# A new order of the steps between graph attention and flow attention, and other engines for two units' subtracts

## The chip, the cores and the metric

The kernel runs on one core of one Trainium2 chip. The metric is the device time of one execution in microseconds (us), as the median of several runs. The engines are TensorE (PE, with its weight load PEld), VectorE (DVE), ScalarE (ACT), GpSimd (POOL) and SyncE (SP), which issues DMAs.

## The reference, cut to what matters

Four graph layers follow each other on `x` (32 batches, 512 nodes, 64 features), each as `x = x + layer(relu(layernorm(x)))`. Layers 0 and 1 multiply with the adjacency matrix and small weights. The change concerns the end of layer 2 and the begin of layer 3:

```python
# layer 2: graph attention
Wh = einsum('bnf,of->bno', h, W)
e = leaky_relu((Wh @ a1)[:, :, None] + (Wh @ a2)[:, None, :], 0.2)
att = softmax(where(adj > 0, e, -9e15), axis=-1)
x = x + elu(einsum('bij,bjo->bio', att, Wh))
# layer 3: flow attention, 8 heads of 128, then one output attention of the same form
h = relu(layernorm(x)) @ W[head]
s = einsum('bnd,bmd->bnm', h, h) * adj
s = where(s == 0, -1e16, s)
out = einsum('bnm,bmd->bnd', softmax(s, axis=2), h) + b
```

## The kernel before

Tensors lie with 128 nodes on the partitions; 512 nodes are C = 4 blocks of 128. Layers 0 to 2 work on pairs of batches, M = 16 pairs. `slot(k)` (line 1207) is one step of a software pipeline over pairs: pair k in layer 0, k-2 in layer 1, k-4 and k-5 in layer 2. When the slots are done, pairs 10 to 15 are still on their way. What is left is issued by `drain()` (line 1315), which follows a list written out by hand, `LAST` (line 1297): each word `name_i` is a step of pair i (or of unit i of layer 3), and the words' order is the order in which PE, DVE and ACT get their instructions (`manual_schedule`, line 1439). POOL and SP are not under it in the drain.

The steps that matter, for pair i of layer 2: `flip`/`ht` transpose and copy; `e1`, `c`, `wh`, `vq` the terms of the scores; `weigh` (L1057); `sc0`, `sc1` the masked scores, four instructions of 128x512 each (L1069: `c`, `mask_t` and the result in SBUF); `acc`, `den` the weighted sums on TensorE (L1082, L1093), `kacc`, `kden` their copies to SBUF, `op`, `dps` the transposes back (L1123, L1118); `read` the quotient (L1136, L1137, L1144); `exp` and `rest` the elu and the addition to x (L1157, L1158, then L905 and two L907 that centre it for the next norm); `osq`, `ovar` square and sum. Layer 1 has `nt1`, `nt1c`, `po1a`, `z`, `nt1b`, `nt1bc`, `po1b`, `x`; norms have `n1`, `n2` (centre), `sq`, `var`, `root` (square root on ACT), `turn` (reciprocal), `relu`.

Layer 3 is a row of units, `flow`: `Heads(b, i)` treats heads 2i and 2i+1 of batch b; the first units are flow[0] = (0,0), flow[1] = (1,0), flow[2] = (0,1), flow[3] = (1,1), and so on. A unit's path: `make_g` (a product on TensorE and a copy on ACT, for two units at once), `scores(r)` for r = 0..3 (L425, two matmuls into PSUM), `maxima(r)` (L440: two VectorE instructions that negate, mask and copy the scores to SBUF and keep the row minimum `top`), `spread_out` and `spread_in` (SP: `top` to DRAM and back, broadcast to all partitions, L447 and L458), `shift(r, engine)` (the subtract of the broadcast: two of 128x512 for r = 0, L468, one of 128x1024 else, L464), `exps(r)` (ACT, L477), `join(1)` and `join(3)` (VectorE, L480: rows 1 and 0, rows 3 and 2 added), `totals` (L498), `values` (L486, into `av`), `recips` and their DMAs, `normalize` (L535). `exps(r)` of an odd r writes into a PSUM tile `e_ps` for units from EARLY = 2 on, and in place for units 0 and 1. `e_ps` and the scores share `ps_s`, a ring of two tiles.

`planned()` (line 777) makes `flow_period(t)`: one period issues steps of some ten units, each at its lag: scores of unit t and t+1, shift and exps of unit t-1, totals and values of t-2, `make_g` of t+2, `features` of later batches. Units 0 and 1 are exempt from the first of these (`t - i >= EARLY`): the list `LAST` issues them, with `topb` in `adj_t`, which layer 2 needs no more. In the kernel before the list holds all of unit 0 and unit 1 up to `j1`, both with GpSimd subtracts, and all pairs to `osq_15`. Behind the list come unit 0's totals, period 1, unit 0's values, period 2, `end_of_gat` (variance and root of pair 15, line 1428) and periods 3 and on. Batch 15's result `o_end` lies in a buffer of the tag `hs3`, its exponential in `pairs_a`.

Of the kernel before, what the change touches and what calls it, by code (L numbers as in the profile page):

```python
# [14 lines left out]
P = 128  # L15
# [7 lines left out]
def fast_form(  # L23
# [340 lines left out]
    class Pair:  # L364
# [17 lines left out]

        def make_gs(self):
            pass
# [88 lines left out]
        def exps(self, r):  # L473
            to = self.joined[r] = self.p[r]
            if r % 2 and self.at >= EARLY:
                to = self.joined[r] = ps_s.tile([P, 2, N], F32, name="e_ps", tag="s")
            nc.scalar.activation(to, self.p[r], AF.Exp, scale=-1.0)  # L477
# [59 lines left out]
    class Heads(Pair):  # L537
# [51 lines left out]
        def make_g(self):  # L589
            if self.b % 2:  # L590
                return
            pss = [acc("g_ps", [P, N]) for k in range(2)]
            for k in range(2):
# [12 lines left out]
                )  # L606
            for k in range(2):
# [169 lines left out]
    def planned(units, products):  # L777
# [7 lines left out]
        def period(t):  # L785
# [4 lines left out]
            now, ahead, last = (unit(i) if t - i >= EARLY else nothing for i in (0, -1, 1))  # L790
            summed = unit(2) if t > 2 else nothing
# [6 lines left out]
            last.exps(0)  # L798
# [6 lines left out]
            last.exps(2)  # L805
# [3 lines left out]
            odd = nc.vector if t == EARLY + 1 else nc.gpsimd  # L809
# [12 lines left out]
            last.shift(1, odd)  # L822
            last.exps(1)
# [7 lines left out]
            last.join(1)  # L831
            last.shift(3, odd)
            last.exps(3)
            unit(5).back_pool()
            unit(-2).make_gs()
            last.join(3)
# [4 lines left out]
            unit(-2).make_g()  # L841
            for step in range(3):
# [43 lines left out]
    with (  # L886
# [110 lines left out]
        class Gat:  # L997
# [134 lines left out]
            def read(self):  # L1132
# [6 lines left out]
                if self.i == LATEST:  # L1139
                    self.sq = early.tile([P, 2, C, F], F32, name="o_end", tag="hs3", bufs=2)  # L1140
# [8 lines left out]
            def exp(self):  # L1149
                self.e = pairs_a.tile([P, 2, C, F], F32, name="e", bufs=1)  # L1150
                nc.scalar.activation(self.e, self.sq, AF.Exp)
# [146 lines left out]
        grow_15 nt1bc_13 flip_12 nt1_14 ht_12 read_10 sc0_11 exp_10 po1b_13 nt1c_14 rest_10  # L1298
        e1_12 wh_12 c_12 po1a_14 vq_12 n1_15 s0_0 z_14 osq_10 sc1_11 sq1_15 x_13 acc_11
        n2_13 var1_15 sq2_13 weigh_12 var2_13 den_11 kacc_11 ovar_10 m0_0 root_0 op_11  # L1300
        nt1b_14 sc0_12 kden_11 turn_0 dps_11 relu1_15 nt1bc_14 s1_0 relu2_13 nt1_15 m1_0
        read_11 sc1_12 exp_11 flip_13 nt1c_15 po1b_14 ht_13 e1_13 rest_11 wh_13 c_13 acc_12
        vq_13 x_14 osq_11 n2_14 den_12 ovar_11 sq2_14 weigh_13 kacc_12 var2_14 s2_0 kden_12
        sc0_13 root_1 dps_12 s3_0 po1a_15 m2_0 op_12 z_15 m3_0 nt1b_15 turn_1 relu2_14
        read_12 sc1_13 flip_14 nt1bc_15 spread_0 s0_1 ht_14 exp_12 po1b_15 e1_14 x_15 acc_13
        rest_12 c_14 n2_15 osq_12 den_13 sh0_0 kacc_13 ovar_12 sq2_15 m0_1 op_13 kden_13
        sh1_0 ex0_0 dps_13 var2_15 s1_1 read_13 root_2 s2_1 m1_1 sh2_0 m2_1 s3_1 period_0
        exp_13 sh3_0 turn_2 ex2_0 wh_14 m3_1 vq_14 relu2_15 spread_1 ex1_0 sc0_14 flip_15
        ht_15 ex3_0 weigh_14 sc1_14 e1_15 wh_15 c_15 vq_15 sh0_1 rest_13 acc_14 sh1_1 ex0_1
        weigh_15 osq_13 j3_0 den_14 kacc_14 sh2_1 ovar_13 ex1_1 op_14 sc0_15 kden_14 dps_14  # L1310
        sh3_1 ex2_1 sc1_15 ex3_1 read_14 j3_1 exp_14 acc_15 rest_14 den_15 kacc_15 j1_0
        osq_14 ovar_14 op_15 kden_15 j1_1 dps_15 read_15 exp_15 rest_15 osq_15
        """

        def drain():
# [84 lines left out]
            for r in range(C):  # L1400
                do[f"s{r}"] = lambda i, r=r: flow[i].scores(r)
                do[f"m{r}"] = lambda i, r=r: flow[i].maxima(r)
                do[f"sh{r}"] = lambda i, r=r: flow[i].shift(r, nc.gpsimd)
# [3 lines left out]
            def spread(i):  # L1407
                flow[i].spread_out()
                flow[i].spread_in()

            do["spread"] = spread
            do["period"] = flow_period
# [15 lines left out]
        def end_of_gat(sp):  # L1428
            sp.add(gat[LATEST])
# [52 lines left out]
    with tc.manual_schedule(  # L1482
# [15 lines left out]
        end_of_gat(unfinished)  # L1498
        for k in range(3, len(flow) + ROOM):
# [563 lines left out]
```

## Time and profile before

| | |
|---|---|
| Median of 3 runs | 2022.88 us (2019.3, 2022.88, 2022.89) |
| The profiled execution, its own time | 2021.3 us |
| Its span, first to last instruction | 2019.4 us |
| Granted TensorE clock, mean | 0.988 |
| PE busy | 1946.5 us (96%) |
| DVE busy | 1747.8 us (87%) |
| POOL busy | 1452.9 us (72%) |
| ACT busy | 1320.8 us (65%) |
| Chain that ended last | PE 79%, POOL 7%, DVE 6%, DMA 4%, ACT 2%, issue 1% |

A line such as `L464` names a line of the kernel before. "Busy" counts an engine's instructions; a matmul that is pipelined counts as busy while it is under way. A timeline row tells start, length, engine, line, operation and tiles, and in brackets how long the engine was idle before and what ended that. The profiler's span is a little shorter than the time of the execution, which also holds what lies ahead of the first and behind the last instruction.

### The profile page before, as it was taken

Reading aid. Unit: us, or ns where it says so; the run is one execution under the profiler, and the core shown is the slowest. Engines: PE = TensorE matmul, PEld = TensorE weight load, DVE = VectorE, ACT = ScalarE, POOL = GpSimd, SP = SyncE. Lnnn points to the kernel's source line nnn. Section 1 sums busy time; section 2 is a strip of 40 time slices with the busy share of each in tenths; the row PEclk is TensorE's granted clock in tenths of the full one; section 3 lists DMA queues with packets and bytes.
Section 4 is the critical chain, followed back from the end, with each engine's and each line's share of the span. In section 5 each row is a group of like instructions: output and inputs, shape, how many; then the busy total and the mean of one; then the engine's idle time right before and its main releaser. Section 6 shows DMA issues by size and latency. Waiting matters only on the chain.

```text
span 2019.4 us, 29031 instructions
## 1 busy us (share of the span) xinstructions
PE 1946.5 (96%) x9338; PEld 729.7 (36%) x9338; DVE 1747.8 (87%) x4104; ACT 1320.8 (65%) x2008; POOL 1452.9 (72%) x837
## 2 busy tenths in 40 slices
PE   7999999868999999999999999999999999999995
PEld 4655554322333333333333333333333333333232
DVE  6799987987889898988988898888888888888994
ACT  3545655446777677777776767777776776766674
POOL 2000000226989999989898989898898888889996
PEclk9999999888999999999999999999999999999998
DMA  4000000002232232323223323332222223222223
GB/s 124 1 1 1 1 1 1 11 12 68 77 79 77 75 85 76 84 71 86 74 77 80 80 70 86 75 75 80 75 70 75 75 76 76 73 77 78 77 75 82
DMA packets 185874, 128.03 MB, mean 63 GB/s; under 512 B 124985, under 2 KB 130273, under 8 KB 185585
## 3 DMA queue, kind: packets, MB, share of 16 engines
q1 hardware_dynamic: 166480, 125.30, 23.2%
q10 hardware_dynamic: 18720, 0.59, 0.5%
q8 instruction: 75, 1.23, 0.3%
q14 instruction: 87, 0.70, 0.1%
q0 software_dynamic: 512, 0.20, 0.1%
HBM read 119.48 MB, written 5.37 MB: 62 GB/s over the span
## 4 chain that ended last, share of the span: by engine, by line
PE 79%; POOL 7%; DVE 6%; DMA 4%; ACT 2%; issue 1%; SPq 0%; ACTq 0%; POOLq 0%; DVEq 0%
PE s_ps L425 22%; PE av L486 20%; PE nt_ps L966 8%; PE tot_ps L498 6%; PE y_ps L616 5%; PE gT_ps L661 5%; PE g_ps L598 3%; POOL p_att L464 3%; PE acc L1082 2%; DMA topb<-top_row 2%; POOL row L464 2%; PE po L988 1%; DVE s L1069 1%; PE den L1093 1%; DVE p_att L440 1%
## 5 line engine op out<-in xcount | busy, mean ns | idle before, releaser
L425 PE MATMUL s_ps<-g,hx 64*128 64x512 f32 x2048 | 519.5, 618 | 12.4 <-DVE p_att L480 5.8
L464 POOL TENSOR_TENSOR row<-row,topb 128x1024 f32<-128x1024 f32 x182 | 430.5, 2388 | 0.0
L464 POOL TENSOR_TENSOR p_att<-p_att,topb 128x1024 f32<-128x1024 f32 x182 | 429.6, 2383 | 0.0
L440 DVE CUSTOM_DVE_ANT_0 p_att<-s_ps,flow_neg 128x512 f32<-128x512 f32 x492 | 310.0, 686 | 43.7 <-PE s_ps L425 42.8
L440 DVE CUSTOM_DVE_ANT_0 row<-s_ps,flow_neg 128x512 f32<-128x512 f32 x496 | 312.5, 685 | 39.1 <-PE s_ps L425 38.9
L425 PEld LDWEIGHTS s_ps<-g,hx 64*128 64x128 f32 x2048 | 176.3, 187 | 323.4 <-DVE top L440 175.9
L468 POOL TENSOR_TENSOR p_att<-p_att,topb 128x512 f32<-128x512 f32 x124 | 155.6, 1277 | 94.4 <-DMA topb<-top_row 80.5
L1211 POOL TENSOR_TENSOR x<-x,bias_b 128x512 f32<-128x512 f32 x16 | 20.3, 1274 | 255.1 <-DVE hn L907 255.1
L468 POOL TENSOR_TENSOR row<-row,topb 128x512 f32<-128x512 f32 x120 | 150.9, 1279 | 63.8 <-DMA topb<-top_row 49.3
L610 ACT COPY g<-g_ps 128x512 f32<-128x512 f32 x128 | 132.1, 1140 | 94.4 <-PE g_ps L598 94.3
L634 DVE SCALAR_TENSOR_TENSOR cat<-y_ps,bh,cat 128x512 f32<-128x512 f32 x256 | 180.1, 745 | 15.1 <-ACT cat L626 13.2
L626 ACT ACTIVATE cat<-y_ps,bh 128x512 f32<-128x512 f32 x256 | 161.1, 681 | 34.3 <-PE y_ps L616 33.8
L477 ACT ACTIVATE row<-row 128x1024 f32<-128x1024 f32 x127 | 134.7, 1060 | 69.3 <-POOL row L468 35.5
L477 ACT ACTIVATE p_att<-p_att 128x1024 f32<-128x1024 f32 x123 | 130.2, 1058 | 69.8 <-POOL p_att L468 35.6
L480 DVE TENSOR_TENSOR p_att<-e_ps,p_att 128x1024 f32<-128x1024 f32 x123 | 145.5, 1198 | 15.8 <-ACT e_ps L477 15.3
L480 DVE TENSOR_TENSOR row<-e_ps,row 128x1024 f32<-128x1024 f32 x121 | 143.2, 1197 | 13.9 <-ACT e_ps L477 13.4
L477 ACT ACTIVATE e_ps<-p_att 128x1024 f32<-128x1024 f32 x123 | 125.7, 1029 | 39.1 <-POOL p_att L464 33.0
L477 ACT ACTIVATE e_ps<-row 128x1024 f32<-128x1024 f32 x121 | 123.5, 1030 | 32.3 <-POOL row L464 26.6
L464 POOL TENSOR_TENSOR adj_p<-adj_p,topb 128x1024 f32<-128x1024 f32 x60 | 142.8, 2380 | 0.0
L616 PE MATMUL y_ps<-o_att,wh_sb 64*128 64x512 f32 x512 | 136.9, 594 | 0.0
L661 PE MATMUL gT_ps<-cat,wo_sb 128*64 128x512 f32 x512 | 131.7, 592 | 0.0
L535 DVE TENSOR_TENSOR o_att<-av,recb 128x512 f32<-128x512 f32 x144 | 99.0, 687 | 25.3 <-DMA recb<-rec_row 24.5
(236 smaller groups left out, 3480.4 us busy)
## 6 DMA issues: line engine op xcount, KB each, us to landing
topb<-top_row SPq DMA_DIRECT2D x284, 256.0 KB
recb<-rec_row SPq DMA_DIRECT2D x288, 128.0 KB
out_dram<-y SPq DMA_DIRECT2D x32, 128.0 KB
x<-in_x_dram SPq DMA_DIRECT2D x3, 1024.0 KB
top_row<-top SPq DMA_DIRECT2D x144, 4.0 KB
parts<-tot SPq DMA_DIRECT2D x144, 4.0 KB
parts<-tot ACTq DMA_DIRECT2D x144, 4.0 KB
rec_row<-rec_flow SPq DMA_DIRECT2D x144, 4.0 KB
```

Of the source, the lines that this page charges most:

```text
L425: nc.tensor.matmul(ps[k], lhsT=x[halves(k), r * P : (r + 1) * P], rhs=g[halves(k), :], start=True, stop=True,)
L440: nc.vector.tensor_tensor_reduce(out=self.p[r][:, k], in0=ps[k], in1=flow_neg[:, r], scale=-1.0, scalar=BIG, op0=OP.add, op1=OP.min, accum ...
L464: engine.tensor_tensor(self.p[r], self.p[r], self.topb, OP.subtract)
L468: engine.tensor_tensor(p, p, self.topb[:, k], OP.subtract)
L477: nc.scalar.activation(to, self.p[r], AF.Exp, scale=-1.0)
L480: nc.vector.tensor_tensor(self.p[r], self.joined.pop(r), self.p[r - 1], OP.add)
L486: nc.tensor.matmul(self.av[halves(k), :], lhsT=self.v(k, j) if j % 2 else self.less_next(k, j), rhs=self.p[j][:, k], start=(j == 0), stop= ...
L616: nc.tensor.matmul(ps, lhsT=wh_sb[halves(k), 2 * self.i + k, :], rhs=self.o[halves(k), :], start=True, stop=True,)
L626: nc.scalar.activation(self.cat[:, k], self.y[k], AF.Identity, bias=bh01[:, h : h + 1], scale=0.01)
L634: nc.vector.scalar_tensor_tensor(self.cat[:, k], self.y[k], bh[:, h : h + 1], self.cat[:, k], op0=OP.add, op1=OP.max,)
L661: nc.tensor.matmul(self.gps[halves(k), :], lhsT=wo_sb[:, h, :], rhs=Heads.cat.pop((self.b + k, h)), start=(h == 0), stop=(h == H - 1),)
L966: nc.tensor.matmul(p, lhsT=lhs(k), rhs=adj_t[:, k, :], start=(k == 0), stop=(k == C - 1))
```

## The change

The list `LAST` is ordered anew. Unit 0's shifts go to VectorE (`sh0_0` to `sh3_0`), unit 1's to GpSimd by `spread_1` itself, and unit 1's exps and odd join leave the list: period 2 issues them (`made = unit(1) if t > 1`). Unit 1's odd exps now write into `e_ps`. `period_0` leaves the list; of its steps `make_g` of unit 2 comes as `gp_2` (matmuls) and `gc_2` (copies), the method being cut in two, and `features(2)` of unit 9 comes behind `end_of_gat`. Pair 15's `rest` and `osq` move from the list into `end_of_gat`, and its exponential gets a buffer of its own (`e_end`). In period 3 the two VectorE subtracts of unit 2 stand ahead of `spread_in`, `normalize` and the next maxima, where they stood behind them.

```diff
--- before.py
+++ after.py
@@ -380,6 +380,9 @@
         def make_g(self):
             pass
 
+        def copy_g(self):
+            pass
+
         def make_gs(self):
             pass
 
@@ -472,7 +475,7 @@
 
         def exps(self, r):
             to = self.joined[r] = self.p[r]
-            if r % 2 and self.at >= EARLY:
+            if r % 2 and self.at:
                 to = self.joined[r] = ps_s.tile([P, 2, N], F32, name="e_ps", tag="s")
             nc.scalar.activation(to, self.p[r], AF.Exp, scale=-1.0)
 
@@ -589,7 +592,7 @@
         def make_g(self):
             if self.b % 2:
                 return
-            pss = [acc("g_ps", [P, N]) for k in range(2)]
+            pss = self.pss = [acc("g_ps", [P, N]) for k in range(2)]
             for k in range(2):
                 u = self.pair[k]
                 u.x = Heads.hx[u.b]
@@ -604,6 +607,11 @@
                     start=True,
                     stop=True,
                 )
+
+        def copy_g(self):
+            if self.b % 2:
+                return
+            pss = self.pss
             for k in range(2):
                 u = self.pair[k]
                 u.g = early.tile([P, N], F32, name="g", bufs=3)
@@ -788,6 +796,7 @@
 
 
             now, ahead, last = (unit(i) if t - i >= EARLY else nothing for i in (0, -1, 1))
+            made = unit(1) if t > 1 else nothing
             summed = unit(2) if t > 2 else nothing
             for r in range(2, C):
                 now.scores(r)
@@ -795,18 +804,20 @@
             unit(6).store()
             unit(4).bias()
             last.shift(0, nc.gpsimd)
-            last.exps(0)
+            made.exps(0)
             summed.totals()
             summed.totals_out(1, nc.scalar)
             u, h = products.get(t - 1, (None, 0))
             if u and h == H - 1:
                 u.keep_product()
             last.shift(2, nc.gpsimd)
-            last.exps(2)
+            made.exps(2)
             for r in range(2, C):
                 now.maxima(r)
             now.spread_out()
-            odd = nc.vector if t == EARLY + 1 else nc.gpsimd
+            if t == EARLY + 1:
+                last.shift(1, nc.vector)
+                last.shift(3, nc.vector)
             summed.totals_out(0, nc.sync)
             now.spread_in()
             for r in range(2):
@@ -819,8 +830,9 @@
             unit(4).back()
             unit(4).y_dve()
             unit(4).back_dve()
-            last.shift(1, odd)
-            last.exps(1)
+            if t != EARLY + 1:
+                last.shift(1, nc.gpsimd)
+            made.exps(1)
             for j in range(C):
                 summed.values(j)
             u, h = products.get(t, (None, 0))
@@ -828,17 +840,19 @@
                 u.product(h)
             unit(2).recips()
             unit(2).recips_out()
-            last.join(1)
-            last.shift(3, odd)
-            last.exps(3)
+            made.join(1)
+            if t != EARLY + 1:
+                last.shift(3, nc.gpsimd)
+            made.exps(3)
             unit(5).back_pool()
             unit(-2).make_gs()
-            last.join(3)
+            made.join(3)
             unit(-3).features(3)
             unit(-2).judge_product()
             unit(1).make_v()
             unit(-4).make_hx()
             unit(-2).make_g()
+            unit(-2).copy_g()
             for step in range(3):
                 for lag, odd in ((step - 7, 0), (step - 11, 1)):
                     u = unit(lag)
@@ -1137,7 +1151,10 @@
                 nc.vector.reciprocal(rec, rec)
 
                 if self.i == LATEST:
-                    self.sq = early.tile([P, 2, C, F], F32, name="o_end", tag="hs3", bufs=2)
+                    self.sq, self.e = (
+                        early.tile([P, 2, C, F], F32, name=n, tag="hs3", bufs=2)
+                        for n in ("o_end", "e_end")
+                    )
                 else:
                     self.sq = work.tile([P, 2, C, F], F32, name="o")
                 o = self.sq
@@ -1147,7 +1164,8 @@
                 )
 
             def exp(self):
-                self.e = pairs_a.tile([P, 2, C, F], F32, name="e", bufs=1)
+                if self.i != LATEST:
+                    self.e = pairs_a.tile([P, 2, C, F], F32, name="e", bufs=1)
                 nc.scalar.activation(self.e, self.sq, AF.Exp)
 
             def grow(self):
@@ -1295,21 +1313,20 @@
 
         LATEST = M - 1
         LAST = """
-        grow_15 nt1bc_13 flip_12 nt1_14 ht_12 read_10 sc0_11 exp_10 po1b_13 nt1c_14 rest_10
-        e1_12 wh_12 c_12 po1a_14 vq_12 n1_15 s0_0 z_14 osq_10 sc1_11 sq1_15 x_13 acc_11
-        n2_13 var1_15 sq2_13 weigh_12 var2_13 den_11 kacc_11 ovar_10 m0_0 root_0 op_11
-        nt1b_14 sc0_12 kden_11 turn_0 dps_11 relu1_15 nt1bc_14 s1_0 relu2_13 nt1_15 m1_0
-        read_11 sc1_12 exp_11 flip_13 nt1c_15 po1b_14 ht_13 e1_13 rest_11 wh_13 c_13 acc_12
-        vq_13 x_14 osq_11 n2_14 den_12 ovar_11 sq2_14 weigh_13 kacc_12 var2_14 s2_0 kden_12
-        sc0_13 root_1 dps_12 s3_0 po1a_15 m2_0 op_12 z_15 m3_0 nt1b_15 turn_1 relu2_14
-        read_12 sc1_13 flip_14 nt1bc_15 spread_0 s0_1 ht_14 exp_12 po1b_15 e1_14 x_15 acc_13
-        rest_12 c_14 n2_15 osq_12 den_13 sh0_0 kacc_13 ovar_12 sq2_15 m0_1 op_13 kden_13
-        sh1_0 ex0_0 dps_13 var2_15 s1_1 read_13 root_2 s2_1 m1_1 sh2_0 m2_1 s3_1 period_0
-        exp_13 sh3_0 turn_2 ex2_0 wh_14 m3_1 vq_14 relu2_15 spread_1 ex1_0 sc0_14 flip_15
-        ht_15 ex3_0 weigh_14 sc1_14 e1_15 wh_15 c_15 vq_15 sh0_1 rest_13 acc_14 sh1_1 ex0_1
-        weigh_15 osq_13 j3_0 den_14 kacc_14 sh2_1 ovar_13 ex1_1 op_14 sc0_15 kden_14 dps_14
-        sh3_1 ex2_1 sc1_15 ex3_1 read_14 j3_1 exp_14 acc_15 rest_14 den_15 kacc_15 j1_0
-        osq_14 ovar_14 op_15 kden_15 j1_1 dps_15 read_15 exp_15 rest_15 osq_15
+        read_10 flip_12 nt1_14 sc0_11 ht_12 exp_10 nt1bc_13 rest_10 e1_12 nt1c_14 po1a_14
+        c_12 wh_12 z_14 sc1_11 po1b_13 osq_10 vq_12 nt1b_14 ovar_10 x_13 grow_15 acc_11
+        nt1bc_14 n1_15 n2_13 sq1_15 var1_15 den_11 sq2_13 weigh_12 kacc_11 var2_13 op_11
+        sc0_12 s0_0 root_0 po1b_14 s1_0 sc1_12 kden_11 dps_11 read_11 turn_0 exp_11 acc_12
+        relu1_15 rest_11 den_12 kacc_12 m0_0 osq_11 ovar_11 op_12 kden_12 nt1_15 x_14 n2_14
+        relu2_13 sq2_14 m1_0 flip_13 nt1c_15 dps_12 ht_13 po1a_15 read_12 s2_0 z_15 var2_14
+        exp_12 nt1b_15 m2_0 root_1 rest_12 e1_13 nt1bc_15 turn_1 po1b_15 osq_12 relu2_14
+        c_13 wh_13 ovar_12 x_15 flip_14 vq_13 n2_15 ht_14 weigh_13 sq2_15 sc0_13 e1_14 wh_14
+        c_14 vq_14 sc1_13 s3_0 var2_15 acc_13 weigh_14 root_2 m3_0 spread_0 den_13 kacc_13
+        turn_2 relu2_15 flip_15 kden_13 sc0_14 gp_2 ht_15 e1_15 gc_2 op_13 sc1_14 dps_13
+        c_15 wh_15 s0_1 vq_15 read_13 sh0_0 exp_13 acc_14 sh1_0 ex0_0 sh2_0 ex1_0 weigh_15
+        den_14 kacc_14 sh3_0 ex2_0 op_14 kden_14 sc0_15 s1_1 ex3_0 dps_14 sc1_15 m0_1 m1_1
+        s2_1 read_14 s3_1 m2_1 acc_15 m3_1 j1_0 spread_1 den_15 j3_0 kacc_15 rest_13 op_15
+        kden_15 dps_15 osq_13 exp_14 ovar_13 read_15 rest_14 exp_15 osq_14 ovar_14
         """
 
         def drain():
@@ -1400,16 +1417,20 @@
             for r in range(C):
                 do[f"s{r}"] = lambda i, r=r: flow[i].scores(r)
                 do[f"m{r}"] = lambda i, r=r: flow[i].maxima(r)
-                do[f"sh{r}"] = lambda i, r=r: flow[i].shift(r, nc.gpsimd)
+                do[f"sh{r}"] = lambda i, r=r: flow[i].shift(r, nc.vector)
                 do[f"ex{r}"] = lambda i, r=r: flow[i].exps(r)
                 do[f"j{r}"] = lambda i, r=r: flow[i].join(r)
 
             def spread(i):
                 flow[i].spread_out()
                 flow[i].spread_in()
+                if i:
+                    for r in (0, 2, 1, 3):
+                        flow[i].shift(r, nc.gpsimd)
 
             do["spread"] = spread
-            do["period"] = flow_period
+            do["gp"] = lambda i: flow[i].make_g()
+            do["gc"] = lambda i: flow[i].copy_g()
             u = turned.pop()
             gat[u.i] = u
             for step in LAST.split():
@@ -1426,6 +1447,8 @@
                     flow_stats[n.i] = n.mean, n.rstd
 
         def end_of_gat(sp):
+            gat[LATEST].grow()
+            gat[LATEST].square()
             sp.add(gat[LATEST])
             sp.root()
             sp.turn()
@@ -1496,6 +1519,7 @@
             flow[0].values(j)
         flow_period(2)
         end_of_gat(unfinished)
+        flow[9].features(2)
         for k in range(3, len(flow) + ROOM):
             flow_period(k)
```

## The prediction

> **What bounds the kernel now.** I read the page's slices first, then busy time by window, then each engine's timeline from 340 to 500 us, then the chain of waits there. Columns of the windows: length, busy time and count of PE, PEld, DVE, ACT and POOL, granted clock, DMA share, GB/s.
>
> ```profile
> 340.00:380.00 40.00, 39.55 (x211) 19.26 (x210) 39.05 (x86) 19.25 (x37) 0.00 (x0) 1.00 0.01 1
> 380.00:400.00 20.00, 14.76 (x69) 6.25 (x69) 17.99 (x25) 8.83 (x13) 10.71 (x5) 0.80 0.07 27
> 400.00:420.00 20.00, 10.67 (x54) 6.17 (x52) 14.46 (x23) 10.78 (x23) 9.77 (x5) 0.67 0.09 28
> 420.00:440.00 20.00, 15.60 (x76) 5.13 (x72) 19.65 (x30) 7.08 (x11) 1.64 (x1) 0.93 0.00 0
> 440.00:460.00 20.00, 14.97 (x72) 4.97 (x72) 15.08 (x42) 8.81 (x18) 1.36 (x2) 1.00 0.11 28
> 460.00:480.00 20.00, 14.94 (x52) 4.37 (x52) 14.82 (x35) 8.68 (x13) 14.27 (x8) 0.74 0.21 54
> ...
> 500.00:520.00 20.00, 20.00 (x96) 6.48 (x96) 17.99 (x44) 13.40 (x20) 16.83 (x11) 1.00 0.29 69
> ```
>
> From 480 us on TensorE is busy all the time, and the chain of waits runs along it, so the end is the moment at which this state begins plus a fixed amount of matmuls. In the drain (340 to 480) TensorE lacks 29 us. VectorE is full until 382 and from 410 to 443. The change touches only this stretch: the order of all five engines is the same before it and from period 4 on.
>
> VectorE is not only full, it is stretched. Its timeline (start, length, operation), first free of GpSimd, then beside it, and GpSimd's own:
>
> ```profile
> 365.82 0.68 DVE L1157 SCALAR_TENSOR_TENSOR x<-o,x 128x512 f32<-128x512 f32 x1
> 368.06 0.76 DVE L907 SCALAR_TENSOR_TENSOR o<-sum,x 128x256 f32<-128x256 f32 x2
> 372.77 2.73 DVE L1069 SCALAR_TENSOR_TENSOR s<-c,q,mask 128x512 f32<-128x512 f32 x4
> ...
> 384.21 1.44 DVE L1157 SCALAR_TENSOR_TENSOR x<-o,x 128x512 f32<-128x512 f32 x1
> 385.76 1.58 DVE L1158 SCALAR_TENSOR_TENSOR x<-e,x 128x512 f32<-128x512 f32 x1
> 387.38 0.69 DVE L905 TENSOR_REDUCE sum<-x 128x8 f32<-128x512 f32 x1
> 388.10 4.24 DVE L907 SCALAR_TENSOR_TENSOR o<-sum,x 128x256 f32<-128x256 f32 x2
> 409.81 6.84 DVE L1069 SCALAR_TENSOR_TENSOR s<-c,q,mask 128x512 f32<-128x512 f32 x4 [5.07 <-ACT q L1041]
> 416.58 0.74 DVE L1057 TENSOR_TENSOR v<-wh_ps,v 128x256 f32<-128x256 f32 x2
> ```
>
> ```profile
> 383.83 2.96 POOL L468 TENSOR_TENSOR row<-row,adj_t 128x512 f32<-128x512 f32 x2 [66.73 <-DMA adj_t<-top_row]
> 386.76 7.79 POOL L464 TENSOR_TENSOR row<-row,adj_t 128x1024 f32<-128x1024 f32 x3
> 410.23 3.13 POOL L468 TENSOR_TENSOR row<-row,adj_t 128x512 f32<-128x512 f32 x2 [15.69 <-DMA adj_t<-top_row]
> ```
>
> An instruction with two tensors in SBUF (L1157, L1158, L907, L1069) ends only 0.3 to 0.6 us after the GpSimd instruction that was running when it came: one passes for each. One with a single tensor (L905) or with one in PSUM (L1057, L440) keeps its time. [...]
>
> The handover ends with TensorE's last long wait, behind unit 2's second join:
>
> ```profile
> 460.51 3.64 PE L425 MATMUL s_ps<-g,hx 64*128 64x512 f32 x8 [3.34 <-DVE top L440]
> 473.41 2.08 PE L425 MATMUL s_ps<-g,hx 64*128 64x512 f32 x4 [2.76 <-DVE p_att L480]
> ```
>
> **The change, part 1: the attention (340.00 to 443.06 before).** From VectorE's first read after its wait (340.00) to the last pair's `o_end` (442.36 + 0.70) it takes 103.1 us. Its work at undisturbed pitch (start to start, rows of 341 to 383 and 424 to 443): 40 L1069 at 0.66 = 26.5; 6 reads (L1136, L1137, L1144) at 1.05 = 6.3; 5 rests (L1157, L1158, L905, two L907) at 2.92 = 14.6; 3 x (L1358 twice) at 0.77 = 2.3; 4 n (L905, two L907) at 1.41 = 5.6; 9 vars (L944) at 0.6 = 5.4; 4 L1057 pairs at 0.66 = 2.6; 8 maxima (two L440 each) at 1.22 = 9.8; 4 joins (L480) at 1.13 = 4.5; 3 rstd at 0.3 and 4 relu (L930 twice) at 0.68 = 3.6. Before, this makes 81.2. Blocking adds (1.44−0.68)+(1.58−0.69)+(4.24−0.76)+(2.20−0.76) = 6.6 beside unit 0's subtracts, and (6.84−2.73)+(6.26−2.73) = 7.6 beside unit 1's. That leaves 103.1 − 81.2 − 14.2 = 7.7 of waits, 5.07 of them at 404.7 behind ScalarE's g copies, hs, table load and exps.
>
> After: unit 0's five subtracts on VectorE. No such VectorE row stands in the trace for `adj_t`; bounds are the all-SBUF join L480 (1.22, pitch 1.13 for 128x1024) and the blocked subtract at 469.38 (1.65): 4.6 to 6.1 for 2 halves and 3 full ones. I take 4.6, for GpSimd has nothing then. `grow_15` (0.6) moves from a wait at 334 into the busy stretch. One rest, one var and unit 1's two joins (5.8) go behind the last read. Work: 81.2 + 4.6 + 0.6 − 5.8 = 80.6. No blocking: GpSimd starts only with `spread_1`.
>
> Which waits stay I found by placing the new order step by step on VectorE, TensorE and ScalarE at these pitches (TensorE: acc 3.6, den 1.85, neighbours 3.6, projections, wh and scores 1.0; table load 1.28). VectorE then has no wait over 0.8: read_11 comes when `den_ps` does (361.4), x_15 when po1b_15 does (379.9), read_13 1.7 after. The new wait, unit 0's subtracts for their DMA, has weigh_15, sc0_15 and sc1_15 queued behind it: `m3_0` ends at 390.6, the landing takes 5.9 (377.94 to 383.83 in the trace), so 396.5; VectorE reaches it at 397.9, with 1.4 to spare. Waits sum to 1.4; I add 1.5 for what the placing misses (0 to 5.07, the largest wait before). 80.6 + 1.4 + 1.5 = 83.5: a lead of 103.1 − 83.5 = **19.6 us**.
>
> **Part 2: the handover (443.06 to 473.41, 30.35 us before).** Unit 1's subtracts now run here. `m3_1` ends 7.5 us before the last read, GpSimd starts 6.0 after it (404.10 to 410.23), 1.5 before that read ends, and needs 11.4 (410.23 to 421.6).
> - To unit 2's `m1`: 5.3 before; now rest_14's L1157, L1158 and two L907 each wait for a GpSimd instruction of 1.5 to 2.8: 12.8.
> - To unit 2's spread: 4.0; now 3.1 (TensorE at half rate, having waited 5 us).
> - Unit 3's first maxima: 2.5; now 2.4.
> - To its spread: 6.7 (a wait of 3.16 for `std`); now recips 0.4, unit 1's two joins 2.4, rest_15 4.1 (unit 2's first GpSimd subtracts fall on it), square, var, table load, std 2.6, maxima 2.4: 11.9. The joins ran inside the attention before (435 to 442); the ring of two `s_ps`/`e_ps` tiles now puts unit 3's scores 2 and 3 and all of TensorE behind them.
> - To the score matmul behind join 3: 11.7 (wait for recb, normalize, then subtract, exp, join twice in a row); now both VectorE subtracts go first: 2.3 + 0.65 + 2.45 + 0.4 + 2.3 = 8.1. The exps end under the maxima.
>
> Sum 38.3, against 30.2: 8.1 given back. Net 19.6 − 8.1 = **11.5 us**. features(2) of unit 9 (1.27, L572) moves behind `std`, where ScalarE waits in any case. The table loads stay 34, SP issues the same DMAs in the same order.
>
> Span 2019.4 − 11.5 = 2007.9; the execution took 2021.3, 1.9 more, so 2009.8. The median of the runs shown (2022.88) is 1.6 above that execution, so it would be 2011.4 on that scale; I say **2010**. Bounds of the gain: with none of part 2's blocking +7.5, with rest_15 blocked by three full subtracts −5, with unit 0's subtracts at 1.65 −1.5, with all of a 5.07 wait −3.6. One of these at a time gives 6 to 19 us, 2002 to 2015, its own range.
>
> A clock row bears on this:
>
> ```profile
> 410.23:421.60 11.37, 6.63 (x25) 3.57 (x26) 11.37 (x8) 4.86 (x10) 11.37 (x5) 0.50 0.01 3
> ```
>
> After waits of 5.66 and 3.49 us TensorE had half its clock here. [...] It speaks against the change where that leaves TensorE waiting 4 to 5 us three times (405, 428, 446 by my placing).
>
> **Rivals.**
> - *The handover is free* (the blocked instructions slip between GpSimd's): 19 us, 2002. For it: VectorE might win the race at the start. Against: between 384 and 395 and between 410 and 423 every such row that came while GpSimd ran was stretched. 0.12.
> - *The lead is given back.* All eight two-tensor instructions of rest_14 and rest_15 behind a full GpSimd instruction: 8 × (2.7 − 0.6) = 16.8 instead of the 8.7 above (7.5 and 1.2), and two waits like those of 0.88 and 0.86 at 382 and 398: 9.8 less, 2020. For it: both rests stand close behind a spread. Against: unit 2's subtracts come after most of rest_15. 0.13.
> - *Slower: TensorE stays at half rate through the handover.* acc_15 to dps_15 (7.5 at full rate) doubles, less 1.5 spare: +6; five pairs of scores on the path +3; the first two steady periods (11.4 and 10.9, y to y) until it warms, +11: 2010 + 20 = 2030. It decides from the point where waits recur in every few us. For it: 0.67 in 400 to 420. Against: after 3.34 us idle, av at 464.07 ran at full rate within 4 us. 0.15.
>
> **How the numbers follow.** Forecast 0.60, free handover 0.12, lead given back 0.13, slower 0.15. The range takes the first three: 2001 to 2020, 0.85 of the chance. A measurement of this kernel can tell 0.2%, 4 us, from no change. Faster by more: 0.60 + 0.12 + 0.04 of the third = 0.76; within: 0.09; slower: 0.15.
>
> **What would show it.** Right: L1069 near 0.75 throughout; `o_end` near 424 instead of 442; VectorE's subtracts of unit 0 near 1.2; L1157 and L907 stretched once, behind the last read; TensorE's last wait near 462 and nothing changed behind it. Wrong: a VectorE wait of more than 2 us before 415, or TensorE waits after 470.

## The result, and the profile after

| | before | after |
|---|---|---|
| Median of 5 runs each, one chip | 2022.88 us (2019.3 to 2023.47) | 2012.36 us (2010.54 to 2014.2) |
| Span of the profiled execution | 2019.4 us | 2010.6 us |
| First read after VectorE's wait to the end of `o_end` | 103.05 us | 83.23 us |
| From there to the first `y_ps` | 36.15 us | 42.53 us |
| First `y_ps` to the end | 1540.2 us | 1540.7 us |

The ratio is 0.9952, 95% interval 0.9937 to 0.9967: 10.5 us faster, where 12.9 were forecast from the same median (2010). The prediction's own sum came to 2011.4 on the scale of that median; the 2010 that it named is 1.4 lower. The last three rows come from timelines; `o_end` is the quotient of pair 15, the last pair, and the first `y_ps` (L616 before, L624 after) is the fixed place behind the handover. In these two profiles the end lies equally far behind the first `y_ps`, as the prediction has it.

Lines moved by 3 to 18: the maxima are L443 now, scores L428, subtracts L471 and L467, masked scores L1083, rests L1175, L1176, L919 and L921, joins L483. The windows of the kernel after, columns as before:

```profile
340.00:380.00 40.00, 39.64 (x195) 18.71 (x196) 34.27 (x72) 18.77 (x32) 0.00 (x0) 1.00 0.00 1
380.00:400.00 20.00, 19.07 (x115) 9.28 (x113) 19.69 (x42) 12.32 (x26) 0.00 (x0) 1.00 0.05 12
400.00:420.00 20.00, 16.18 (x81) 7.05 (x82) 19.35 (x41) 8.82 (x15) 0.00 (x0) 0.91 0.04 16
420.00:440.00 20.00, 14.01 (x70) 4.31 (x66) 12.85 (x24) 3.73 (x7) 10.33 (x5) 0.96 0.09 28
440.00:460.00 20.00, 13.40 (x42) 3.63 (x40) 17.63 (x39) 14.83 (x27) 5.67 (x4) 0.76 0.14 41
460.00:480.00 20.00, 19.60 (x88) 6.81 (x88) 17.30 (x44) 13.79 (x19) 15.14 (x9) 0.94 0.28 81
```

GpSimd has nothing until 426, and VectorE does 41 instructions between 400 and 420 where it did 23. TensorE now lacks time mainly between 400 and 460 (3.8, 6.0 and 6.6 us in the three windows), and is nearly full from 460 instead of 480. VectorE's timeline in the attention, with unit 0's subtracts and the last two sets of masked scores:

```profile
396.25 5.39 DVE L1083 SCALAR_TENSOR_TENSOR s<-c,q,mask 128x512 f32<-128x512 f32 x8
...
402.60 1.28 DVE L471 TENSOR_TENSOR row<-row,adj_t 128x512 f32<-128x512 f32 x2
403.81 2.35 DVE L467 TENSOR_TENSOR row<-row,adj_t 128x1024 f32<-128x1024 f32 x2
...
406.74 1.22 DVE L467 TENSOR_TENSOR row<-row,adj_t 128x1024 f32<-128x1024 f32 x1
408.47 5.39 DVE L1083 SCALAR_TENSOR_TENSOR s<-c,q,mask 128x512 f32<-128x512 f32 x8 [0.51 <-PE den L1107]
```

Nothing is stretched: 5.39 for eight, 1.2 for a full subtract. The handover, VectorE's timeline and then GpSimd's:

```profile
427.25 0.80 DVE L1175 SCALAR_TENSOR_TENSOR x<-o,x 128x512 f32<-128x512 f32 x1
428.14 1.57 DVE L1176 SCALAR_TENSOR_TENSOR x<-e,x 128x512 f32<-128x512 f32 x1
429.75 0.69 DVE L919 TENSOR_REDUCE sum<-x 128x8 f32<-128x512 f32 x1
436.58 0.69 DVE L443 CUSTOM_DVE_ANT_0 p_att<-s_ps,flow_neg 128x512 f32<-128x512 f32 x1 [6.14 <-POOL adj_p L467]
437.19 0.76 DVE L921 SCALAR_TENSOR_TENSOR o<-sum,x 128x256 f32<-128x256 f32 x2
```

```profile
426.22 2.95 POOL L471 TENSOR_TENSOR row<-row,adj_t 128x512 f32<-128x512 f32 x2 [108.03 <-DMA adj_t<-top_row]
429.13 2.80 POOL L467 TENSOR_TENSOR adj_p<-adj_p,adj_t 128x1024 f32<-128x1024 f32 x1
431.90 2.35 POOL L467 TENSOR_TENSOR row<-row,adj_t 128x1024 f32<-128x1024 f32 x1
434.21 2.33 POOL L467 TENSOR_TENSOR adj_p<-adj_p,adj_t 128x1024 f32<-128x1024 f32 x1
```

One instruction is clearly stretched (L1176, 1.57 us; the same one of pair 13 took 0.69). Then VectorE stands for 6.14 us: unit 2's first maxima wait, by a semaphore, until GpSimd's last subtract ends at 436.54, though they read nothing of it. TensorE's waits in this stretch:

```profile
414.52 3.96 PE L428 MATMUL s_ps<-g,hx 64*128 64x512 f32 x8 [3.02 <-DVE top L443]
...
438.61 4.62 PE L428 MATMUL s_ps<-g,hx 64*128 64x512 f32 x12 [5.57 <-DVE top L443]
...
447.59 3.21 PE L428 MATMUL s_ps<-g,hx 64*128 64x512 f32 x8 [1.96 <-DVE row L483]
456.65 3.78 PE L428 MATMUL s_ps<-g,hx 64*128 64x512 f32 x8 [4.23 <-DVE top L443]
```

Eight score matmuls take 1.99 us at full rate (427.47, clock 1.00). Over these four rows the granted clock was 0.57, 0.65, 0.66 and 0.50, as the third rival has it. Behind the last wait full rate was back within 6 us, at 462.4 (clock 1.00 over the matmuls at 462.44).

The first read came at 344.10, 4.1 us later than in the profile of before (340.00), although nothing ahead of it was changed. One group of matmuls explains most of that, in TensorE's timeline first of before, then of after:

```profile
321.99 3.70 PE L966 MATMUL nt_ps<-adj_t,hn 128*128 128x512 f32 x8 [2.94 <-DVE unsound L272]
```

```profile
323.08 6.71 PE L980 MATMUL nt_ps<-adj_t,hn 128*128 128x512 f32 x8 [2.96 <-DVE unsound L272]
```

The wait is the same, but behind it the granted clock was 1.00 over the row of before and 0.55 over the row of after.

### The profile page after: what moved, and what is told of

It reads as the page before. It is cut to its first block, busy times and chain, and to the rows that moved or that the text cites. A ratio compares the mean times of both kernels' runs of the same rounds, so it can differ in the third digit from the quotient of the medians.

```text
span 2010.6 us, 29032 instructions
## 1 busy us (share of the span) xinstructions
PE 1950.3 (97%) x9338; PEld 728.6 (36%) x9338; DVE 1740.0 (87%) x4109; ACT 1322.4 (66%) x2008; POOL 1442.0 (72%) x832
## 4 chain that ended last, share of the span: by engine, by line
PE 78%; POOL 7%; DVE 6%; DMA 5%; ACT 2%; issue 2%; SPq 0%; ACTq 0%; POOLq 0%; DVEq 0%
PE s_ps L428 21%; PE av L489 20%; PE nt_ps L980 8%; PE tot_ps L501 6%; PE y_ps L624 5%; PE gT_ps L669 5%; PE g_ps L601 3%; PE acc L1096 3%; POOL row L467 2%; POOL p_att L467 2%; DMA topb<-top_row 2%; PE po L1002 1%; DVE row L443 1%; PE den L1107 1%; DMA top_row<-top 1%
## 5 line engine op out<-in xcount | busy, mean ns | idle before, releaser
L428 PE MATMUL s_ps<-g,hx 64*128 64x512 f32 x2048 | 521.1, 618 | 19.9 <-DVE top L443 13.2
L467 POOL TENSOR_TENSOR row<-row,topb 128x1024 f32<-128x1024 f32 x182 | 429.9, 2383 | 0.0
L467 POOL TENSOR_TENSOR p_att<-p_att,topb 128x1024 f32<-128x1024 f32 x182 | 429.9, 2384 | 0.0
L443 DVE CUSTOM_DVE_ANT_0 p_att<-s_ps,flow_neg 128x512 f32<-128x512 f32 x492 | 310.4, 687 | 50.0 <-PE s_ps L428 43.4
L443 DVE CUSTOM_DVE_ANT_0 row<-s_ps,flow_neg 128x512 f32<-128x512 f32 x496 | 312.6, 686 | 38.9 <-PE s_ps L428 38.5
L428 PEld LDWEIGHTS s_ps<-g,hx 64*128 64x128 f32 x2048 | 177.2, 187 | 330.0 <-DVE top L443 186.8
L471 POOL TENSOR_TENSOR p_att<-p_att,topb 128x512 f32<-128x512 f32 x124 | 156.2, 1281 | 75.4 <-DMA topb<-top_row 63.6
L642 DVE SCALAR_TENSOR_TENSOR cat<-y_ps,bh,cat 128x512 f32<-128x512 f32 x256 | 180.1, 746 | 15.1 <-ACT cat L634 13.4
L471 POOL TENSOR_TENSOR row<-row,topb 128x512 f32<-128x512 f32 x120 | 151.0, 1280 | 58.7 <-DMA topb<-top_row 50.9
L483 DVE TENSOR_TENSOR p_att<-e_ps,p_att 128x1024 f32<-128x1024 f32 x123 | 145.3, 1198 | 13.2 <-ACT e_ps L480 12.9
L483 DVE TENSOR_TENSOR row<-e_ps,row 128x1024 f32<-128x1024 f32 x122 | 144.2, 1197 | 13.4 <-ACT e_ps L480 13.2
L467 POOL TENSOR_TENSOR adj_p<-adj_p,topb 128x1024 f32<-128x1024 f32 x60 | 143.1, 2385 | 0.0
L624 PE MATMUL y_ps<-o_att,wh_sb 64*128 64x512 f32 x512 | 136.8, 594 | 0.0
L980 PE MATMUL nt_ps<-adj_t,hn 128*128 128x512 f32 x256 | 119.0, 609 | 4.8 <-DVE unsound L272 3.0
```

Of the source, the lines that this page charges most:

```text
L428: nc.tensor.matmul(ps[k], lhsT=x[halves(k), r * P : (r + 1) * P], rhs=g[halves(k), :], start=True, stop=True,)
L443: nc.vector.tensor_tensor_reduce(out=self.p[r][:, k], in0=ps[k], in1=flow_neg[:, r], scale=-1.0, scalar=BIG, op0=OP.add, op1=OP.min, accum ...
L467: engine.tensor_tensor(self.p[r], self.p[r], self.topb, OP.subtract)
L471: engine.tensor_tensor(p, p, self.topb[:, k], OP.subtract)
L483: nc.vector.tensor_tensor(self.p[r], self.joined.pop(r), self.p[r - 1], OP.add)
L624: nc.tensor.matmul(ps, lhsT=wh_sb[halves(k), 2 * self.i + k, :], rhs=self.o[halves(k), :], start=True, stop=True,)
```

## The experiments

Totals scatter by 2 to 8 us between runs of one kernel, so each profile is also read at three places: the first read after VectorE's wait, the end of `o_end`, the first `y_ps`. Kernel changes are against the kernel after, except for "old order", which is against the kernel before. Median ratios are to the kernel before on the same chip. Its median was 2027.7 us on the chip of "new order", "old order", "96 bytes free" and "unit 1 on VectorE"; 2028.6 on that of "once more", "period 3", "end of pair 15" and "L272, L273"; and 2023.4 on that of the other four.

| | first read to `o_end` | to first `y_ps` | sum | ratio, 95% interval |
|---|---|---|---|---|
| before | 103.05 | 36.15 | 139.20 | |
| after | 83.23 | 42.53 | 125.76 | 0.9952, 0.9937 to 0.9967 |
| after, once more | 85.07 | 43.21 | 128.28 | 0.9930, 0.9917 to 0.9942 |
| new order, unit 0 on GpSimd | 85.86 | 42.22 | 128.08 | 0.9942, 0.9928 to 0.9956 |
| old order, unit 0 on VectorE | 98.99 | 37.09 | 136.08 | 0.9988, 0.9977 to 0.9999 |
| 96 bytes free | 84.91 | 39.47 | 124.38 | 0.9927, 0.9914 to 0.9940 |
| unit 1 on VectorE | 85.03 | 40.37 | 125.40 | 0.9925, 0.9913 to 0.9938 |
| period 3 in old order | 85.06 | 47.64 | 132.70 | 0.9956, 0.9943 to 0.9969 |
| end of pair 15 split | 85.01 | 41.45 | 126.46 | 0.9933, 0.9921 to 0.9946 |
| odd exps in place | 84.92 | 42.73 | 127.65 | 0.9941, 0.9928 to 0.9954 |
| L272, L273 early | 84.80 | 42.88 | 127.68 | 0.9927, 0.9915 to 0.9940 |
| three edits together | 83.57 | 40.39 | 123.96 | 0.9913, 0.9900 to 0.9926 |
| and the rest later | 83.42 | 47.81 | 131.23 | 0.9933, 0.9921 to 0.9944 |
| and the rest last | 83.40 | 48.69 | 132.09 | 0.9947, 0.9934 to 0.9960 |

**The kernel after, once more.** 

> The changed kernel itself, once more, beside the runs that follow. From the first read to the first y_ps 125.8 us again, plus or minus 1.7 by the chance of the granted clock (the spread of the same stretch up to den of pair 14 in two other kernels); the end 1540 to 1545 us behind that; ratio to before 0.993 to 0.997.

First read at 340.01 (the matmul group took 3.70 this time), so the 4.1 us were chance. In the attention VectorE waited 2.17 us for `den` of pair 14 instead of 0.51. The other kernels with the same list up to `o_end` took 83.4 to 85.1, so that stretch has a chance of about 1.8 us of its own, and edits are compared with 128.28 and 125.76 both. The sum of 128.28 lies outside the 125.8 plus or minus 1.7 that was expected; the end (1542.9 us behind the first `y_ps`) and the ratio came as expected. VectorE's row behind that wait:

```profile
406.02 5.39 DVE L1083 SCALAR_TENSOR_TENSOR s<-c,q,mask 128x512 f32<-128x512 f32 x8 [2.17 <-PE den L1107]
```

**Engine and order apart.** Only unit 0's subtracts change their engine; unit 1's ran on GpSimd in the kernel before too. The new order with unit 0 on GpSimd:

```diff
-                do[f"sh{r}"] = lambda i, r=r: flow[i].shift(r, nc.vector)
+                do[f"sh{r}"] = lambda i, r=r: flow[i].shift(r, nc.gpsimd)
```

> New order, but unit 0's five subtracts back on GpSimd. Theory (the order keeps GpSimd's subtracts off the busy stretch, and the change of engine for unit 0 spares the rest of the blocking): GpSimd runs them from about 10 us behind unit 0's spread, VectorE waits some 3 to 4 us for den of pair 13 where its subtracts stood, and two or three groups of masked scores of the last pair are stretched from 2.7 to 4 to 6 us; the attention (first read to the end of o_end) takes 86 to 87.5 us in place of 83.2, the whole 2015 to 2017. Rival (stretched rows have another cause than GpSimd): every group of masked scores keeps 0.66 to 0.75 us an instruction and the attention stays at 83 to 84 us, 2012.

VectorE's timeline, then GpSimd's:

```profile
402.80 0.76 DVE L1071 TENSOR_TENSOR v<-wh_ps,v 128x256 f32<-128x256 f32 x2 [0.24 <-ACT q L1055]
408.34 7.50 DVE L1083 SCALAR_TENSOR_TENSOR s<-c,q,mask 128x512 f32<-128x512 f32 x8 [4.78 <-PE den L1107]
```

```profile
400.94 2.94 POOL L471 TENSOR_TENSOR row<-row,adj_t 128x512 f32<-128x512 f32 x2 [82.90 <-DVE s L1083]
403.83 7.48 POOL L467 TENSOR_TENSOR row<-row,adj_t 128x1024 f32<-128x1024 f32 x3
```

The mechanism is as expected: a wait of 4.78 us where the subtracts stood, and eight masked scores stretched from 5.39 to 7.50 while GpSimd ran (to 411.3). The size is smaller, 85.86 in place of 86 to 87.5. At the first `y_ps` it equals the second profile of the kernel after (128.08 and 128.28). The median, 2016.7 us where before takes 2027.7, is not told apart from the kernel after by its ratio.

The old order with unit 0 on VectorE:

```diff
-                do[f"sh{r}"] = lambda i, r=r: flow[i].shift(r, nc.gpsimd)
+                do[f"sh{r}"] = lambda i, r=r: flow[i].shift(r, nc.vector if i == 0 else nc.gpsimd)
```

> The old order, with unit 0's five subtracts on VectorE and nothing else changed. Theory of the prediction (engine and order each give a part): the attention loses 6.6 us of blocking and gains 4.6 us of subtracts, so 100 to 102 us in place of 103.1, and the whole comes 1 to 3 us below the kernel before; the 5 us wait before 405 stays. Rival (the change of engine is the whole gain): 2012 to 2014.

VectorE's timeline:

```profile
389.33 1.29 DVE L468 TENSOR_TENSOR row<-row,adj_t 128x512 f32<-128x512 f32 x2
...
406.53 4.77 DVE L1069 SCALAR_TENSOR_TENSOR s<-c,q,mask 128x512 f32<-128x512 f32 x4 [4.62 <-ACT q L1041]
```

The 5 us wait stays (4.62), and unit 1's subtracts still stretch the masked scores (four in 4.77 here, the next four in 8.35). The attention gets 4.1 us shorter, 1 us more than the 100 to 102 that were expected allow: waits of 0.86 and 0.40 us at 399 and 401 are gone too. The first `y_ps` comes 3.1 us earlier, the median falls by 0.12% (some 2.5 us). So of some 13 us at the first `y_ps`, the whole new order without the change of engine brings 11.1 (139.20 − 128.08); this holds the new place of unit 2's subtracts in period 3, which is tried by itself below. The change of engine alone brings 3.1, and in the new order between nothing and 2.3, which chance hides.

**The wait for GpSimd.** In the layout of the compiled kernel the pool of unit 2's rows, opened where earlier pools have ended, begins 96 bytes a partition below the end of `adj_t`, whose upper half holds unit 1's broadcast.

```diff
+    gap = ctx.enter_context(tc.tile_pool(name="gap", bufs=1))
+    gap.tile([P, 24], F32, name="gap")
```

> 96 bytes a partition are left free ahead of the pool of unit 2's rows, so that the first of them no longer overlaps the upper half of adj_t, where unit 1's broadcast lies; nothing else. Theory (unit 2's first maxima wait for GpSimd's last subtract of unit 1 because of that overlap, by memory alone): the 6.14 us wait of VectorE behind o_end is gone, the two L921 of pair 14 are stretched by GpSimd instead, the second maxima end 9 to 10.5 us behind o_end in place of 13.0, and the whole comes 2 to 4 us below 2012.4. Rival (the prediction's reading, blocking sets it): 12.8 to 13.0 us behind o_end, no change of time.

VectorE's timeline:

```profile
430.70 0.68 DVE L443 CUSTOM_DVE_ANT_0 p_att<-s_ps,flow_neg 128x512 f32<-128x512 f32 x1
431.31 3.75 DVE L921 SCALAR_TENSOR_TENSOR o<-sum,x 128x256 f32<-128x256 f32 x2
434.99 0.68 DVE L443 CUSTOM_DVE_ANT_0 p_att<-s_ps,flow_neg 128x512 f32<-128x512 f32 x1
```

The wait is gone, the two L921 are stretched from 0.76 to 3.75 instead. The second maxima end 9.8 us behind `o_end` in place of 13.0, and the first `y_ps` comes 3.1 to 3.7 us earlier in the handover. The wait was by memory alone. The median is not told apart from the kernel after (0.9927 and 0.9930), so the 2 to 4 us that were expected of the whole are not shown.

The other way out of it, unit 1's subtracts on VectorE:

```diff
-        kden_15 dps_15 osq_13 exp_14 ovar_13 read_15 rest_14 exp_15 osq_14 ovar_14
+        kden_15 dps_15 osq_13 exp_14 ovar_13 read_15 sh0_1 sh2_1 sh1_1 sh3_1 rest_14 exp_15 osq_14 ovar_14
...
-                if i:
-                    for r in (0, 2, 1, 3):
-                        flow[i].shift(r, nc.gpsimd)
```

> Unit 1's five subtracts on VectorE, right behind the last read, so that GpSimd has none in the handover. Theory (the wait for GpSimd's last subtract costs more than VectorE's own 4.6 to 5.3 us): subtracts end 5 us behind o_end, the rest of pair 14 is undisturbed (2.9 us) and comes with no wait, the second maxima end 10 to 10.8 us behind o_end in place of 13.0: 2 to 3 us below 2012.4. Rival (VectorE has no room there): 13 us or more behind o_end, 2012 to 2015.

The five subtracts took 424.58 to 429.27, the rest of pair 14 was undisturbed (L1175 0.68, L1176 0.69), the second maxima ended 10.4 us behind `o_end`: as expected. So VectorE's own 4.7 us are only 0.6 to 0.9 dearer than GpSimd's blocking without the overlap. The median is not told apart here either (0.9925).

**Period 3.**

```diff
-            if t == EARLY + 1:
-                last.shift(1, nc.vector)
-                last.shift(3, nc.vector)
+            odd = nc.vector if t == EARLY + 1 else nc.gpsimd
...
+            last.shift(1, odd)
...
+            last.shift(3, odd)
```

> Unit 2's two VectorE subtracts back behind the next maxima in period 3, everything else as in the changed kernel. Theory (the prediction's last piece, 8.1 in place of 11.7): subtract, exp and join come twice in a row again, the piece from unit 3's spread to the scores behind unit 2's second join grows by 2.5 to 3.6 us, first y_ps 2.5 to 3.6 later. Rival (the exps end under the maxima in either order): less than 0.5 us.

VectorE's timeline here, then in the kernel after:

```profile
460.21 1.22 DVE L467 TENSOR_TENSOR p_att<-p_att,topb 128x1024 f32<-128x1024 f32 x1
...
462.60 1.22 DVE L483 TENSOR_TENSOR p_att<-e_ps,p_att 128x1024 f32<-128x1024 f32 x1 [0.85 <-ACT e_ps L480]
463.74 1.25 DVE L467 TENSOR_TENSOR p_att<-p_att,topb 128x1024 f32<-128x1024 f32 x1
466.08 1.23 DVE L483 TENSOR_TENSOR p_att<-e_ps,p_att 128x1024 f32<-128x1024 f32 x1 [1.09 <-ACT e_ps L480]
```

```profile
457.74 2.35 DVE L467 TENSOR_TENSOR p_att<-p_att,topb 128x1024 f32<-128x1024 f32 x2
...
463.37 2.32 DVE L483 TENSOR_TENSOR p_att<-e_ps,p_att 128x1024 f32<-128x1024 f32 x2
```

Subtract, exp and join come twice in a row again, and VectorE waits for each exp. The handover is 4.4 us longer (5.1 against the first profile), more than the 3.6 at most: TensorE also waits 2.36 us between the two pairs of scores. This is the one edit by itself that the median tells from the kernel after on the same chip: 2020.35 us against 2013.34. If the parts add up, the order of two subtracts makes 4.4 to 5.1 us of the 11.1 that the new order brings at the first `y_ps`.

**The end of pair 15.**

```diff
-            sp.add(gat[LATEST])
-            sp.root()
-            sp.turn()
-            keep_stats(sp)
+            behind[3] = [
+                lambda: sp.add(gat[LATEST]), sp.root, sp.turn, lambda: keep_stats(sp)
+            ]
```

> Variance, root and reciprocal of pair 15 go to the end of period 3, its rest stays before that period; everything else as in the changed kernel. Theory (VectorE's wait for the variance, the table load and the root holds back unit 3's maxima): these start 2.0 to 3.0 us earlier behind the rest of pair 15, the first y_ps 1 to 2.5 us earlier. Rival (the two table loads of the root now stand ahead of exps that are due): no change or up to 1.5 us later.

Unit 3's last maxima start right behind the rest (450.15) and not 2.5 us behind it (455.35 against 452.82 in the kernel after). The first `y_ps` comes 1.1 to 1.8 us earlier, near the lower end. The median is not told apart.

Unit 1's odd exps in place:

```diff
-            if r % 2 and self.at:
+            if r % 2 and self.at >= EARLY:
```

> Unit 1's odd exps in place instead of in the ring of two PSUM tiles that the scores use too; everything else as in the changed kernel. Theory of the prediction (the ring puts unit 3's scores 2 and 3 and all of TensorE behind unit 1's joins): these scores start 2 to 3.5 us earlier, but unit 3's maxima wait for the root of pair 15 in any case, so the first y_ps moves by less than 0.7 us. Rival (the ring itself is on the path): 1 to 2.5 us earlier.

Unit 3's last scores start 2.7 us earlier behind `o_end` than in the second profile of the kernel after (445.51 with no wait), TensorE then waits 7.20 us for unit 3's maxima, and the first `y_ps` gains 0.5 at most. The ring delays those scores, as the prediction had it, but the root of pair 15 hides it.

**The front.** L272 and L273 go between the read and the rest of the pair before:

```diff
             while turned:
-                turned.pop().end()
-            if k == 7 + 2 * C:
-                judge()
+                v = turned.pop()
+                v.read()
+                v.exp()
+                if k == 7 + 2 * C:
+                    judge()
+                v.rest()
```

> In the last of the main loop's steps, ahead of all that was changed, the two small VectorE instructions L272 and L273 go ahead of a wait of VectorE's instead of behind it, so that TensorE's 2.95 us wait for L272 at 320 is gone; everything else as in the changed kernel. Theory (the scatter between runs comes largely from whether the clock halves in that wait): the eight matmuls behind it take 3.7 us in every run, the first read comes at 339 to 340 us, the median falls by 1 to 3 us, and the runs lie within 2.5 us of one another. Rival (the scatter comes from elsewhere): first read as before, the same spread of 3 to 7 us.

The wait is gone, the matmuls take 3.60, the first read comes at 338.5. But the median is that of the kernel after on the same chip (2013.36 and 2013.34), so the second half of the expectation fell. The five runs lie within 2.6 us, the six of the kernel after within 7.6: a hint of where the scatter comes from, not more.

**Together, and one step further.** "Three edits together" are the free bytes, the split end and the early L272. The next two also move pair 15's rest (with `before_back[3] = [gat[LATEST].grow]`, run behind unit 4's first maxima, or at the head of `behind[3]`), its square and features(2) of unit 9.

> Three of the edits together on the changed kernel: 96 bytes left free ahead of unit 2's rows, variance, root and reciprocal of pair 15 at the end of period 3, L272 and L273 early. If they add up: from the end of o_end to the first y_ps 43.2 - 3.5 - 1.8 = 38 us, first read at 338.5, the median 2007 to 2010 on a chip where the changed kernel has 2013. If the start of unit 3's maxima is held by TensorE or a join instead, 39.5 and 2010 to 2012.

> As the one before, and pair 15's rest (L1175, L1176, L919, two L921) behind unit 4's first maxima in period 3, its square, variance, root and features(2) of unit 9 at the end of period 3. Theory (VectorE's order sets the handover: what isn't due goes behind what TensorE waits for): unit 3's maxima start within 2.5 us of unit 1's joins, first y_ps 34 to 36.5 us behind o_end, 2005 to 2008. Rival (the rest then runs beside unit 3's GpSimd subtracts, is stretched to 6 to 8 us, and unit 5's scores or hx wait for it): first y_ps earlier, but 2 to 4 us of it lost between 465 and 520, no better than the one before.

> As the one before, with pair 15's rest too at the end of period 3, behind unit 2's joins. Theory: first y_ps another 2 to 3 us earlier than with the rest behind unit 4's maxima, 2003 to 2007. Rival (hs of batch 4 waits for o_end's buffer and TensorE for hx): TensorE waits 2 to 6 us behind 465 and the time is that of the one before or worse.

The first gives 2006.29 us, the lowest ratio of all. Its interval lies below that of the kernel after on its first chip and overlaps that on the second. On its own chip the kernel after was not run; the kernel with the odd exps in place, whose handover is that of the kernel after within 0.5 us, took 2012.34 there (2008.9 to 2014.62, against 2001.8 to 2007.95). The handover was 40.39, not 38. VectorE's timeline shows why, with GpSimd's behind it:

```profile
441.57 1.65 DVE L1179 SCALAR_TENSOR_TENSOR x<-e_end,x 128x512 f32<-128x512 f32 x1
...
443.97 3.13 DVE L924 SCALAR_TENSOR_TENSOR o_end<-sum,x 128x256 f32<-128x256 f32 x2
```

```profile
441.01 3.33 POOL L471 TENSOR_TENSOR p_att<-p_att,topb 128x512 f32<-128x512 f32 x2 [9.80 <-PE s_ps L428]
444.31 2.52 POOL L467 TENSOR_TENSOR p_att<-p_att,topb 128x1024 f32<-128x1024 f32 x1
```

The rest came just as unit 2's subtracts did and took 6.2 us (440.86 to 447.03), 4.2 with the split alone. The other two lose: with the rest behind unit 4's maxima, VectorE and TensorE have these rows:

```profile
444.49 5.20 DVE L467 TENSOR_TENSOR p_att<-p_att,topb 128x1024 f32<-128x1024 f32 x2
...
455.78 4.21 DVE L926 SCALAR_TENSOR_TENSOR o_end<-sum,x 128x256 f32<-128x256 f32 x2
```

```profile
461.47 3.78 PE L428 MATMUL s_ps<-g,hx 64*128 64x512 f32 x8 [5.79 <-DVE p_att L483]
```

Unit 3's last maxima did start 0.1 us behind the joins. But the subtracts that follow then ran beside GpSimd's (5.20 in place of 2.35), the rest too (7.3 us), and TensorE waited 5.79 us; with the rest last, 7.78 for unit 4's last maxima. The rival had it, at a higher price than it said. In both of these kernels all four instructions of the rest of pair 14 were stretched, as the prediction had it. VectorE with the rest behind unit 4's maxima:

```profile
421.10 1.79 DVE L1180 SCALAR_TENSOR_TENSOR x<-o,x 128x512 f32<-128x512 f32 x1
423.00 2.66 DVE L1181 SCALAR_TENSOR_TENSOR x<-e,x 128x512 f32<-128x512 f32 x1
...
426.90 3.73 DVE L926 SCALAR_TENSOR_TENSOR o<-sum,x 128x256 f32<-128x256 f32 x2
```

Unit 2's second maxima ended 11.9 and 11.8 us behind `o_end`, where they had ended 9.8 with the free bytes alone and 9.7 with the three edits.

## Why the prediction was right, and where it was not

**The attention** was forecast at 83.5 and took 83.2 (85.1 in the second profile). Its parts hold: waits 0.57 + 0.21 + 0.51 + 0.70 = 2.0, so work 81.2 (80.6 forecast). Unit 0's subtracts took 1.28 + 2.35 + 1.22 = 4.85, near the lower bound taken. Their wait for the DMA, forecast with 1.4 us to spare, never showed. By the same accounting the work is as much as before (81.2 each), so the 19.8 us are the blocking of 14.2 and some 5.7 of waits.

**The handover's pieces** were forecast at 12.8, 3.1, 2.4, 11.9 and 8.1. The timeline gives 13.0 (to 440.37, the end of unit 2's second maxima), 3.2, 2.5, 11.7 and 8.3 (to about 466.1, the second half of the scores at 465.12). So the sum is 38.7 for 38.3.

**The first piece was right for a wrong reason.** The prediction said that four instructions of the rest of pair 14 each wait for a GpSimd instruction. One was, L1176 by 0.9 us. What decided was not in the sum: the wait for GpSimd's last subtract, made by an overlap of 96 bytes, and VectorE's queue, which holds the two L921 behind that wait. With the overlap gone, the forecast mechanism is the one at work, and the piece takes 9.7 and 9.8 us in the two profiles in which three of the four instructions are stretched and 11.8 and 11.9 in the two in which all four are. So its own price was 1 to 3 us too high. What decides between three and four was not looked into. That the piece still came out at 13.0 for 12.8 is luck. The bound of "none of part 2's blocking, +7.5" was never reached.

**The net.** At the first `y_ps` the gain is 13.4 us in the first profile (19.8 less 6.4) and 10.9 in the second, 11.5 forecast; the first profile lost 4.1 of it ahead of the change, 3.0 of them in the one group of matmuls with the lower clock.

**The signs.** The masked scores kept 0.66 to 0.75 us each, unit 0's subtracts took 1.2, and `o_end` came at 427.3 (423.2 without the 4.1) for 424. Other signs failed. TensorE's last long wait ended at 456.7, not near 462, and the two L921 of pair 14 were not stretched (0.76 us for both). A wait of VectorE of more than 2 us before 415 was named as a sign of being wrong: it stands in the second profile (2.17 at 406), whose gain is nevertheless 10.9.

**The rivals.** *The handover is free*: refuted; it is 6.4 us longer than before, and 3.3 longer with the 96 bytes free (39.5 against 36.2). *The lead is given back*: not here, where the rest of pair 15 lost only 1.3 us beside unit 2's subtracts, but its mechanism is real: placed behind unit 4's first maxima, the same rest took 7.3 us for 4.2, and TensorE waited 5.8. *Slower, TensorE at half rate*: the waits came (3.02, 5.57, 1.96, 4.23) and the clock fell behind each, to 0.50 to 0.66 over the matmuls that follow, but not for long behind the last one: it is 0.94 between 460 and 480, and the end lies 1540.7 us behind the first `y_ps`, 1540.2 before. No run shows the 11 us that this rival puts on the first two steady periods: in the kernel after they took 11.45 and 10.72 us from `y_ps` to `y_ps` (469.86, 481.31, 492.03), and the clock was 1.00 from 480 to 500.

What stays open is why stretches that no edit touched differ by up to 6 us from chip to chip and run to run: first `y_ps` to the end took 1540 to 1546 us in the fourteen profiles.

## What to carry to other kernels

Where two engines block one another, first ask when the second one's work is due, and only then which engine should do it: here the whole new order brought 11 us at the first `y_ps`, some 4 to 5 of them from the place of two subtracts of VectorE's, and changing the engine of unit 0's brought 0 to 3. That the rest of the 11 comes from unit 1's subtracts, which now run behind the attention, was not tried by itself. A wait on an engine whose data the waiting instruction doesn't read can be a wait for memory: the one of 6.14 us here was gone with 96 bytes left free. Look for the tiles that touch. And in a kernel whose runs scatter, compare stretches between fixed places of the timeline, since two of the best edits here moved such a stretch by 2 to 4 us and the median by nothing that could be told.

## What the runs showed of the hardware

The same wait of 2.94 to 2.96 us ahead of the matmuls at 322 left them at 3.70 us in six of the ten profiles that have it, made them 5.2 in two and 6.7 in two (granted clock 0.55 over the 6.71 us, 1.00 over 3.70). What decides between these was not shown. The clock also fell behind the 2.76 us ahead of the row at 473.41 of the kernel before, where it was 0.50 and four score matmuls took 2.08 us for 1.13.

How much blocking costs went by when the two engines met: a rest takes 2.9 us undisturbed (421.98 to 424.90 for pair 13), and pair 15's took 4.2, 6.2 or 7.3 in three orders.
